# A two-layer transformer with routed experts on one core: second attention in groups of two steps, gates turned, side work in small pieces

## The chip, the core and the metric

The kernel is one program on one core of a Trainium2 chip. The metric is the time of one execution on the device, in microseconds (us). The core has five instruction streams that matter here: TensorE (PE, with its weight loads shown apart as PEld), VectorE (DVE), ScalarE (ACT), GpSimd (POOL) and SyncE (SP, which here issues DMAs only). Each runs its own instructions in order; they meet by semaphores. Results of TensorE go to banks of PSUM, 128 partitions by 512 f32 values each, and a bank can be written again once its reader is through.

## The reference

The input x has 4 batches of 1024 tokens, 256 wide, f32. Two layers follow each other, each `x = x + attention(layernorm(x))` and `x = x + ffn(layernorm(x))`.

The first layer has windowed attention (16 heads of 16, window 64) and a mixture of 8 routed SwiGLU experts, two per token by softmax of `x @ gate_w + gate_b`, beside two shared experts. The second layer is the one that most of the change is about:

```python
def _L1_attn_ref(x, wq, bq, wk, bk, wv, bv, wo, bo, gamma, beta):
    Q = (x @ wq + bq).reshape(B * H, S, D)      # B=4, H=16, S=1024, D=16
    K = (x @ wk + bk).reshape(B * H, S, D)
    V = (x @ wv + bv).reshape(B * H, S, D)
    attn = softmax(einsum('bqd,bkd->bqk', Q, K) / sqrt(D))
    out = einsum('bqk,bkd->bqd', attn, V).reshape(B, S, 256) @ wo + bo + x
    return layernorm(out) * gamma + beta

def _L1_ffn_ref(x, gate_w, experts):
    gates = sinkhorn(einsum('bnd,de->bne', x, gate_w))   # 8 rounds
    vals, idx = top_k(swapaxes(gates, -1, -2), 128)      # 128 tokens per expert and batch
    # x[idx] @ experts[e], times the gate value, put back in the tokens' rows (set), else 0
```

Since the reshape is not followed by a transpose, one "head" of 1024 rows by 16 is 64 token rows in 16 chunks of 16 columns. There are 64 such heads; the kernel takes them in 32 pairs.

## The kernel before

**Stages.** First attention, then the feed-forward part of layer one, then the second attention with the start of the second feed-forward part hidden in it, then a tail: the rest of the routing, the experts and the way back. A tile is 128 tokens (32 tiles, `NT`), a unit four tiles (8 units, `NU`).

**Second attention.** The loop at L2145 runs over steps `s`, eight key tiles (`KT`) for each of 32 pairs of heads (`p`), and one step more. A step does, in this order:

- two halves of `scores` (L1840), one for each 512 query columns. A half takes two banks, one for each of the two heads. It issues two matmuls of `k_st` by `q_st`, with 64 rows each, and two that subtract the row maxima (`minus` by `top_st`). ScalarE then turns each bank into exponentials (L1858), which go into one of six slots of `wide`.
- after each half, one part of `maxima` (L1790) for the step `AHEAD` = 12 later: two matmuls of `q_st` by `k_st`, and their row maxima on VectorE. The first part (`kk` = 0) uses a double bank and one reduction (L1808), the second two single banks and two reductions (L1811). When a pair of heads has all its maxima, `max_rows` (L1816) transposes them, and SyncE stores them to DRAM (`tops_d`) and loads them back as `top_st`.
- the `sums` (L1863) of the step before: 16 matmul instructions with values `v_t` as 32-column weights, all into one accumulator bank (`acc`). These have a tile form of 128 by 32, the scores and maxima 64 by 128.
- `some` (L2008), twice: side work, out of queues of generators. A call advances `between` and `aside` by a piece, then the first of `outs`, `projects`, `gating` that has one, and if it had one (or the flag is set) `sort`.
- at the first key tile, a copy of the accumulator on ScalarE (`oT`, L2175), and a new job in `outs`.

The banks of this stage are `open_banks(one=5, two=1, acc=1)` (L2143): five single ones, one double, one accumulator. Side work takes its banks from the single ones too (`misc_bank`).

**Side work.** `put_out` (L1878) is the output side of one pair: transposes of `oT`, a reciprocal and a product on VectorE that give `ctx`, transposes of that and a copy `cT` on ScalarE, the output projection, and the sum `y` (L1910 on VectorE, L1913 on GpSimd, L1914 on VectorE). A piece ends at each `yield 1`; `yield 0` ends a turn without work. `project` (L1690 and on) computes Q and K of a unit, 512 columns at a time into a pair of banks, stores them to DRAM, from where `load` brings them as `q_st` and `k_st`. `values` does four heads per piece. `finish` is the layernorm after a group of tiles (`TOGETHER`). `gate_steps` computes the gates of the second feed-forward part, `share_steps` the Sinkhorn rounds, `choose_steps` (queue `sort`) the choice of 128 tokens per expert for the first half of the batches: 16 rounds of three VectorE operations. `ranks` then scatters the chosen places into DRAM (`rank_d`), 16 times on GpSimd; `rank` is read back after the loop.

**What sets the order.** In the loop, `on_tensor` (L79) ties each TensorE instruction to the one before, so TensorE runs in the order in which the program is written. `issue_after` puts an instruction behind another in the order of issue and adds no wait. The other engines' order follows from a scheduler that honours these ties.

**Gates.** Both layers' gates are computed with the 128 tokens of a tile as weights and the 8 columns of the gate matrix moving (`gate`, and the end of `gate_steps`):

```python
mm_on(ps[:, j * E : (j + 1) * E], lhsT=xT[:, kc, :], rhs=gw1[:, kc, :], ...)
```

Of the kernel before, what the change touches and what calls it, by code (L numbers as in the profile page):

```python
# [18 lines left out]
P = 128  # L19
# [20 lines left out]
def two_layers(  # L40
# [95 lines left out]
    def one_bank():  # L136

        if "one" in sets:
            return lone_bank("one")
        turns.append(0)  # L140
        return acc_bank() if len(turns) % 2 else misc_bank()
# [41 lines left out]
    first_w.append(first_pool.tile([P, NF, D], F32, name="first2"))  # L183
    gw = first_pool.tile([P, 2, E], F32, name="gw")
    gb = first_pool.tile([P, E], F32, name="gb")
# [33 lines left out]

    def gate(u: int):  # L220
        ps = one_bank()
        for j in range(UT):
            for kc in range(2):
                mm_on(
                    ps[:, j * E : (j + 1) * E],
                    lhsT=wide[:, u, kc, j * P : (j + 1) * P],
                    rhs=gw[:, kc, :],
                    start=(kc == 0),
                    stop=(kc == 1),
                )  # L230
        nc.vector.tensor_tensor(
            logits[:, u * UT : (u + 1) * UT],
            ps[:, : UT * E].rearrange("p (j e) -> p j e", j=UT),
            gb.unsqueeze(1).to_broadcast([P, UT, E]),
            ALU.add,
        )
# [65 lines left out]
    with ExitStack() as lc:  # L302
# [28 lines left out]
        nc.scalar.dma_start(out=wo_t, in_=w_out.rearrange("(k p) e -> p k e", p=P))  # L331
        nc.scalar.dma_start(out=gw, in_=gate0_w.rearrange("(k p) e -> p k e", p=P))
        nc.scalar.dma_start(out=gb, in_=gate0_b.partition_broadcast(P))
# [458 lines left out]

    gw1 = fpool.tile([P, 2, E], F32, name="gw1")
    nc.sync.dma_start(out=gw1, in_=gate1_w.rearrange("(k p) e -> p k e", p=P))

# [447 lines left out]
    def gate_steps(i0: int, i1: int, bank, lag: int):  # L1243

        std = small.tile([P, NT], F32, tag="std", name="std")
        nc.scalar.activation(std[:, i0:i1], mv_all[:, i0:i1, 1], AF.Sqrt, bias=eps_t)
        yield from wait(lag)
        nc.vector.reciprocal(rstd_all[:, i0:i1], std[:, i0:i1])
        yield from wait(lag)
        xns = []  # L1250
        for t in range(i0, i1):
            xn = gpool.tile([P, D], F32, tag="xng", name="xng", bufs=4)
            last_xn[:] = [
                (nc.gpsimd if lag else nc.vector)
                .tensor_scalar(
                    xn, x_t[t], mv_all[:, t, 0:1], rstd_all[:, t : t + 1], ALU.subtract, ALU.mult
                )
                .ins
            ]
            nc.gpsimd.dma_start(out=xn_d[t // TB][(t % TB) * P : (t % TB + 1) * P, :], in_=xn)  # L1260
            xns.append(xn)
            yield 0
        yield from wait(2 * lag)
        xTs = []
        for j in range(0, i1 - i0, 2):
            pair = xns[j : j + 2]
            ps = bank()
            for h, xn in enumerate(pair):
                for kc in range(2):
                    c = (2 * h + kc) * P  # L1270
                    turn_on(ps[:, c : c + P], xn[:, kc * P : (kc + 1) * P], ident)
            xT = gpool.tile([P, 4, P], F32, tag="xTg", name="xTg")
            n = 2 * len(pair)
            nc.scalar.copy(xT[:, :n, :].rearrange("p k t -> p (k t)"), ps[:, : n * P])
            xTs += [xT[:, 2 * h : 2 * h + 2, :] for h in range(len(pair))]
            yield 1
        yield from wait(lag)
        ps = bank()
        for j, xT in enumerate(xTs):
            for kc in range(2):  # L1280
                mm_on(
                    ps[:, j * E : (j + 1) * E],
                    lhsT=xT[:, kc, :],
                    rhs=gw1[:, kc, :],
                    start=(kc == 0),
                    stop=(kc == 1),
                )
        nc.vector.tensor_scalar(
            gates[:, i0:i1, :],
            ps[:, : (i1 - i0) * E].rearrange("p (j e) -> p j e", e=E),  # L1290
            CLIP,
            None,
            ALU.max,
        )
        yield 1

    def share_steps(g: int, bank, lag: int):
# [4 lines left out]
        for _ in range(8):  # L1302
# [15 lines left out]
            nc.vector.tensor_tensor(mine, mine, rsum.to_broadcast([P, GT, E]), ALU.mult)  # L1318
            yield 1

# [299 lines left out]
    with ExitStack() as lc:  # L1620
# [68 lines left out]

        def project(u: int):  # L1690

# [22 lines left out]
            for n, w_t in enumerate(wqk_t):  # L1714
                ps = bank_pair()
                for g in range(2):
                    for kc in range(2):
                        mm_on(
                            ps[g],
                            lhsT=w_t[:, kc, g * P : (g + 1) * P],  # L1720
                            rhs=xnT[:, kc, :],
                            start=(kc == 0),
                            stop=(kc == 1),
                        )
                split = apool.tile([P, 2, 2, UN], F32R, tag="split", name="split")
                for g in range(2):
                    bias = b_col[:, 2 * n + g : 2 * n + g + 1]
                    src = ps[g]
                    nc.scalar.activation(split[:, 0, g, :], src, AF.Identity, bias=bias)
                    nc.vector.scalar_tensor_tensor(  # L1730
                        split[:, 1, g, :], src, bias, split[:, 0, g, :].bitcast(F32),
                        ALU.add, ALU.subtract,
                    )

# [7 lines left out]
                halves[u, n] = d  # L1742
                yield 1

        def values(u: int):
# [4 lines left out]
            nc.gpsimd.memset(v_t.rearrange("p h k c -> p (h k) c")[:, :, DH:], 1.0)  # L1750
            for hq in range(HU // 4):
                ps = misc_bank()
                for hh in range(4):
                    t0 = (4 * hq + hh) * HN

                    for kc in range(2):
# [8 lines left out]
                nc.vector.tensor_tensor(  # L1765
                    v_t[:, 4 * hq : 4 * hq + 4, :, :DH],
                    ps.rearrange("p (h k d) -> p h k d", k=8, d=DH),
                    bv_b.to_broadcast([P, 4, 8, DH]),
                    ALU.add,
                )  # L1770
                yield 1
            vals[u] = v_t
# [17 lines left out]
        def maxima(p: int, j: int, kk: int, tops):  # L1790

            q_st, k_st = q_ring[p % RING], k_ring[p % RING]
            if "one" in sets and kk:
                whole, sc = [], bank_pair()
            else:
                two = two_banks().rearrange("p (h c) -> p h c", h=2)
                whole, sc = [two], [two[:, 0], two[:, 1]]
# [80 lines left out]
        def put_out(i: int, oT):  # L1878
# [16 lines left out]
            )  # L1895
            yield 1
            yield 0
# [4 lines left out]
            nc.scalar.copy(cT.rearrange("p k t -> p (k t)"), ps[:, :D])  # L1902
            yield 1
            yield 0
# [10 lines left out]
            ys.append(y)  # L1915
            yield 1
            if i in TOGETHER:
# [89 lines left out]

        def some(idle: bool):  # L2008

            with ExitStack() as behind:  # L2010
                for ins in newest.values():
                    behind.enter_context(tc.issue_after(ins))
                step(between)
                step(aside)
                if step(outs) or step(projects) or step(gating) or idle:
                    step(sort)

# [68 lines left out]
        def stacks():  # L2086
            roots(0, UT)
            yield
            for did in project(0):
                if did:  # L2090
                    yield
# [50 lines left out]
        before, oT_ps = None, None  # L2142
        open_banks(one=5, two=1, acc=1)  # L2143
        in_turn.append("all")
        for s in range(NP * KT + 1):  # L2145
            p, k = divmod(s, KT)
            if k == 0:
# [7 lines left out]
                if p % UT == 3 and p + 5 < NP:  # L2155
                    all_of(projects)
                    projects.append(project(p // UT + 2))
            if k == 1:
                oT_ps = acc_bank()
            pts = []  # L2160
            due = list(noted)
            noted.clear()
            for half in range(2 if p < NP else 0):
                pts.append(scores(p, k, half))
                maxima_step(s + AHEAD, half)
            for half in range(2 if s else 0):
                sums(*divmod(s - 1, KT), half, before, oT_ps)
            for n in due:
                max_rows(n, top_parts.pop(n))
            for half in range(2):  # L2170
                some(half == 0 and k % 4 == 0)
            before = pts
            if k == 0 and s:
# [4 lines left out]
                )  # L2178
                outs.append(put_out(p - 1, oT))
        in_turn.clear()  # L2180
        open_pairs()
# [172 lines left out]
```

## Time and profile before

| what | value |
|---|---|
| time, three runs | 2254.3, 2247.34, 2251.69 us; median 2251.69 |
| the profiled execution | 2264.11 us; span 2262.3 us |
| mean granted TensorE clock in it | 0.958 |
| first attention | 0 to 336 us, 336 long |
| first layer's feed-forward part | 336 to 1110 us, 774 long |
| second attention, to its last sum | 1110 to 2108 us, 998 long |
| tail | 2108 to 2262 us, 154 long |

All times in the tables of the profile come from one execution, taken by the profiler. Busy time is the union of an engine's instructions; "granted clock" is the TensorE clock that the chip allowed, as a share of full speed. A timeline line gives the start, the length from the first start to the last end, the engine, the source line (L86 and L93 are those of the helper that issues TensorE's instructions, so go by the names of the tiles), the tile written and those read, the shapes and the number of instructions, and in brackets the idle time before and who ended it. In a line of a DMA queue, the first word after the queue is the source line.

### The profile page before, as it was taken

To read this page: it belongs to the slowest core of one execution; us is meant where nothing else is said; L and a number is where in the kernel's file an instruction comes from. 1 tells how busy PE (TensorE), PEld (TensorE's weight loads), DVE (VectorE), ACT (ScalarE), POOL (GpSimd) and SP (SyncE) were. 2 spreads that over 40 slices of the span, in tenths; PEclk is the share of its full clock that TensorE was granted. 3 is DMA by queue.
4 is the path that set the end of the run, shared out by engine and by line. 5 is a ranking of instruction groups with operands and counts; after the bars stand their busy time and mean duration, and the time that the engine had idled before them with its cause. 6 is when DMAs were issued, how large, how long until landed. Compare 5 with 4: busy or idle time off the path is not lost.

```text
span 2262.3 us, 50241 instructions
## 1 busy us (share of the span) xinstructions
PE 2085.9 (92%) x19890; PEld 1378.9 (61%) x19890; DVE 1357.9 (60%) x2702; ACT 997.3 (44%) x1898; POOL 651.8 (29%) x862
## 2 busy tenths in 40 slices
PE   7999999999999999997999999999999999998564
PEld 4777776555788888853555555555555555554341
DVE  6676654522222222245887777777777889994483
ACT  3554542111222222221266666767666656667241
POOL 3656541442000000023421222221131212125555
PEclk9999999999999999998999999999999999999676
DMA  4211106113276677633343113132312122100235
GB/s 146 56 44 45 47 12 199 54 65 128 74 234 223 216 234 227 221 97 84 82 109 69 46 46 70 49 76 49 77 44 63 39 60 47 49 21 12 85 98 163
DMA packets 207015, 212.76 MB, mean 94 GB/s; under 512 B 90024, under 2 KB 166088, under 8 KB 206780
## 3 DMA queue, kind: packets, MB, share of 16 engines
q1 hardware_dynamic: 183996, 169.46, 26.6%
q0 software_dynamic: 11552, 29.72, 4.3%
q10 hardware_dynamic: 11232, 10.37, 1.3%
q8 instruction: 158, 2.59, 0.5%
q14 instruction: 77, 0.63, 0.1%
HBM read 140.70 MB, written 56.96 MB: 87 GB/s over the span
## 4 chain that ended last, share of the span: by engine, by line
PE 72%; DVE 12%; issue 6%; POOL 3%; ACT 3%; DMA 2%; SPq 1%; another core or an unknown queue 0%; ACTq 0%; POOLq 0%; DVEq 0%
PE one L86 32%; PE two L86 12%; PE acc L86 10%; PE two L82 7%; PE misc L86 5%; DVE tops L1811 3%; DVE tops L1808 3%; PE misc L82 2%; PE acc L82 2%; ACT wide L1858 1%; POOL yr L2046 1%; POOL xg L1465 1%; DVE cur L1348 1%; PE two L1531 1%; POOL yr L1584 1%
## 5 line engine op out<-in xcount | busy, mean ns | idle before, releaser
L1858 ACT ACTIVATE wide<-one 128x512 f32<-128x512 f32 x1024 | 529.8, 603 | 233.1 <-PE one L86 225.1
L1808 DVE TENSOR_REDUCE tops<-two 128x2 f32<-128x1024 f32 x268 | 325.4, 1216 | 68.5 <-PE two L86 62.0
L1811 DVE TENSOR_REDUCE tops<-one 128x1 f32<-128x512 f32 x488 | 312.9, 679 | 14.7 <-PE one L86 14.6
L86 PE MATMUL acc<-wide,v_t 128*32 128x256 f32 x4096 | 282.4, 393 | 2.5 <-ACT wide L1858 2.1
L86 PE MATMUL two<-xbT,w_t 128*128 128x256 f32 (+1 forms) x1280 | 253.6, 356 | 1.7 <-ACT xbT L1148 1.4
L86 PE MATMUL one<-q_st,k_st 64*128 64x512 f32 x1024 | 243.9, 451 | 2.8 <-ACT wide L1858 1.7
L86 PEld LDWEIGHTS two<-xbT,w_t 128*128 128x128 f32 x1280 | 221.6, 190 | 29.2 <-ACT xbT L1148 1.8
L1181 DVE SCALAR_TENSOR_TENSOR glu_b<-two,b_blk,act_b 128x256 f32<-128x256 f32 (+1 forms) x160 | 72.7, 454 | 244.0 <-ACT act_b L1174 244.0
L86 PE MATMUL one<-top_st,minus 64*128 64x512 f32 x1024 | 215.0, 399 | 2.6 <-DMA top_st<-tops_d 2.6
L1174 ACT ACTIVATE act_b<-two,b_blk 128x256 f32<-128x256 f32 (+1 forms) x160 | 71.9, 450 | 295.1 <-PE two L86 162.6
L86 PE MATMUL one<-k_st,q_st 64*128 64x512 f32 x488 | 174.2, 457 | 29.9 <-ACT wide L1858 21.8
L86 PEld LDWEIGHTS acc<-wide,v_t 128*32 128x32 f32 x4096 | 108.4, 110 | 116.2 <-issue 63.9
L86 PEld LDWEIGHTS one<-q_st,k_st 64*128 64x128 f32 x1024 | 104.7, 186 | 97.2 <-ACT wide L1858 41.7
L271 ACT ACTIVATE act<-two,bT 128x512 f32<-128x512 f32 x60 | 41.2, 687 | 263.9 <-PE two L82 258.4
L86 PEld LDWEIGHTS one<-k_st,q_st 64*128 64x128 f32 x488 | 86.2, 186 | 111.4 <-ACT wide L1858 77.8
L2046 POOL DMA_INDIRECT yr<-ys_d,slot x64 | 61.9, 968 | 222.1 <-DMA ys_d<-yb 80.5
L86 PE MATMUL misc<-w_t,glu_b 128*128 128x256 f32 x552 | 125.6, 379 | 0.0
L82 PE MATMUL two<-wide,w_t 128*128 128x512 f32 x256 | 118.0, 616 | 4.1 <-DVE tops L1808 3.1
L1231 POOL TENSOR_TENSOR x<-x,sb_b 128x256 f32<-128x256 f32 x32 | 23.2, 725 | 336.0 <-DVE glu_b L1181 336.0
L601 POOL TENSOR_SCALAR_AFFINE_SELECT pT<-pT 64x512 f32<-64x512 f32 x128 | 84.0, 656 | 111.9 <-ACT pT L591 109.8
L1913 POOL TENSOR_TENSOR y<-y,wide 128x256 f32<-128x256 f32 x32 | 23.3, 729 | 303.1 <-DVE y L1910 270.6
L86 PEld LDWEIGHTS one<-top_st,minus 64*128 64x128 f32 x1024 | 102.3, 188 | 12.5 <-DMA top_st<-tops_d 2.9
(411 smaller groups left out, 3429.0 us busy)
## 6 DMA issues: line engine op xcount, KB each, us to landing
w_t<-in_L_ffn_rw_dram SPq DMA_DIRECT2D x120, 512.0 KB
halves<-split SPq DMA_DIRECT2D x64, 256.0 KB
q_st<-halves SPq DMA_DIRECT2D x128, 128.0 KB
k_st<-halves SPq DMA_DIRECT2D x256, 64.0 KB
xb<-xs_d SPq DMA_DIRECT2D x31, 256.0 KB
ys_d<-yb ACTq DMA_DIRECT2D x31, 256.0 KB
xs_d<-zeros SPq DMA_DIRECT2D x5, 1536.0 KB
b_t<-in_L_ffn_rb_dram SPq DMA_DIRECT2D x40, 128.0 KB
```

Source lines behind the costliest of these rows:

```text
L82: return do(*args, **kw)
L86: done = do(*args, **kw)
L271: nc.scalar.activation(act, ps[0], AF.Silu, bias=bT[0][:, f, e : e + 1])
L601: nc.gpsimd.affine_select(out=part, in_=part, compare_op=ALU.is_ge, fill=0.0, base=0, pattern=[[0, 8], [1, WIN]], channel_multiplier=-1,)
L1174: nc.scalar.activation(act[:, :cols], ps[:, ff * cols : (ff + 1) * cols], AF.Silu, bias=b_blk[0][:, f, n : n + 1],)
L1181: nc.vector.scalar_tensor_tensor(glu[:, f, :cols], ps[:, 512 + ff * cols : 512 + (ff + 1) * cols], b_blk[1][:, f, n : n + 1], act[:, :cols ...
L1231: nc.gpsimd.tensor_tensor(x_t[m], x_t[m], sb3_b, ALU.add).ins, newest_glu[0]
L1808: last = nc.vector.tensor_reduce(tops[:, :, j, kk], whole[0], AX.X, ALU.max)
L1811: last = nc.vector.tensor_reduce(tops[:, hh, j, kk : kk + 1], sc[hh], AX.X, ALU.max)
L1858: newest["scalar"] = nc.scalar.activation(pt[:, hh * 512 : (hh + 1) * 512], sc[hh], AF.Exp).ins
L1913: nc.gpsimd.tensor_tensor(y, y, bo_b, ALU.add)
L2046: ga = nc.gpsimd.indirect_dma_start(out=yr[:, :], out_offset=None, in_=ys_d[:, :], in_offset=bass.IndirectOffsetOnAxis(ap=slots[k][:, i : ...
```

## The change

- **Gates turned.** The gate matrices `gw` and `gw1` are widened to 32 columns with zeros and become the weights; the tokens move. Four tiles take the four 32-column strips of TensorE, each writing 32 partitions of one bank (`gates_across`). ScalarE copies the result to SBUF, and one TensorE transpose turns it back (`gates_down`).
- **All banks single.** The stage opens `one=7, acc=1`; both parts of `maxima` take two single banks, with two reductions.
- **Groups of two steps.** The loop advances two steps at a time: first half of step one, maxima, `max_rows` if due, `some` once, second half of step one, two parts of maxima, the sums of the two steps before in one run (32 instructions), the copy `oT` where due, first half of step two, maxima, second half of step two.
- **Small pieces.** Each `yield` gives a size instead of 1. `project` works in pieces of 256 columns with one bank each, `values` in pieces of two heads. `some` takes up to four pieces, and no more once their sizes reach 1.2; `sort` moves at the first of its four turns, and at the third if more than 0.8 is spent. In the preparation before the loop `project(0, 1)` keeps the former size.

```diff
-    gw1 = fpool.tile([P, 2, E], F32, name="gw1")
-    nc.sync.dma_start(out=gw1, in_=gate1_w.rearrange("(k p) e -> p k e", p=P))
+    gw1 = fpool.tile([P, 2, 32], F32, name="gw1")
+    nc.vector.memset(gw1, 0.0)
+    nc.sync.dma_start(out=gw1[:, :, :E], in_=gate1_w.rearrange("(k p) e -> p k e", p=P))
...
+    def gates_across(ps, w, tokens):
+        for kc in range(2):
+            for j, of in enumerate(tokens):
+                mm_on(ps[32 * j : 32 * j + 32, :P], lhsT=w[:, kc, :], rhs=of(kc),
+                    start=(kc == 0), stop=(kc == 1), skip_group_check=True)
+        across = small.tile([P, P], F32, tag="across", name="across")
+        rows = slice(0, 32 * len(tokens))
+        nc.scalar.copy(across[rows], ps[rows, :P])
+        return across
+
+    def gates_down(ps, across, n: int):
+        rows = slice(0, 32 * n)
+        turn_on(ps[:, rows], across[rows], ident[rows, rows])
+        return ps[:, rows].rearrange("p (j c) -> p j c", c=32)[:, :, :E]
...
-        def project(u: int):
+        def project(u: int, parts: int = 2):
...
-                ps = bank_pair()
-                for g in range(2):
-                    for kc in range(2):
-                        mm_on(ps[g], ..., rhs=xnT[:, kc, :], ...)
+                pair = bank_pair() if parts == 1 else None
...
+                    for part in range(parts):
+                        cols = slice(part * UN // parts, (part + 1) * UN // parts)
+                        src = pair[g] if pair else misc_bank()[:, cols]
+                        for kc in range(2):
+                            mm_on(src, ..., rhs=xnT[:, kc, cols], ...)
...
+                        if parts > 1:
+                            yield 0.85
...
-            for hq in range(HU // 4):
+            for hp in range(HU // 2):
                 ps = misc_bank()
-                for hh in range(4):
+                for hh in range(2):
...
-                yield 1
+                yield 0.85
...
         def maxima(p: int, j: int, kk: int, tops):
-            if "one" in sets and kk:
+            if "two" not in sets:
                 whole, sc = [], bank_pair()
...
         def put_out(i: int, oT):   # after ctx, after cT, after y
-            yield 1
+            yield 0.45
...
-            yield 1
+            yield 0.25
...
-            yield 1
+            yield 0.85
...
-        def some(idle: bool):
-            with ExitStack() as behind:
-                for ins in newest.values():
-                    behind.enter_context(tc.issue_after(ins))
-                step(between)
-                step(aside)
-                if step(outs) or step(projects) or step(gating) or idle:
-                    step(sort)
+        def some():
+            spent = 0
+            for turn in range(4):
+                with ExitStack() as behind:
+                    for ins in newest.values():
+                        behind.enter_context(tc.issue_after(ins))
+                    step(between)
+                    step(aside)
+                    if spent < 1.2:
+                        spent += step(outs) or step(projects) or step(gating)
+                    if turn == 0 or (turn == 2 and spent > 0.8):
+                        step(sort)
...
-        open_banks(one=5, two=1, acc=1)
+        open_banks(one=7, acc=1)
         in_turn.append("all")
-        for s in range(NP * KT + 1):
+        for s in range(0, NP * KT + 1, 2):
...
-            for half in range(2 if p < NP else 0):
-                pts.append(scores(p, k, half))
-                maxima_step(s + AHEAD, half)
-            for half in range(2 if s else 0):
-                sums(*divmod(s - 1, KT), half, before, oT_ps)
+            half_step(0, 0)
+            maxima_step(s + AHEAD, 0)
             for n in due:
                 max_rows(n, top_parts.pop(n))
-            for half in range(2):
-                some(half == 0 and k % 4 == 0)
+            some()
+            half_step(0, 1)
+            maxima_step(s + AHEAD, 1)
+            maxima_step(s + 1 + AHEAD, 0)
+            if s:
+                for j in range(2):
+                    pb, kb = divmod(s - 2 + j, KT)
+                    if kb == 0:
+                        oT_ps = acc_bank()
+                    for half in range(2):
+                        sums(pb, kb, half, before[j], oT_ps)
             before = pts
             if k == 0 and s:
                 oT = work.tile([P, 4, 2, HN], F32, tag="oT", name="oT1", bufs=2)
...
                 outs.append(put_out(p - 1, oT))
+            half_step(1, 0)
+            maxima_step(s + 1 + AHEAD, 1)
+            half_step(1, 1)
```

`half_step(j, half)` appends `scores(p, k + j, half)` to the results of step `j` as long as `p < NP`.

## The prediction

> **What bounds the kernel now.** I read the page first, then the busy time by stage, then the timeline of single steps in the stage that the change rewrites, engine by engine, and last the waits of the SyncE queue near the end.
>
> ```profile
> span 2262.3 us, 50241 instructions
> ...
> PE 2085.9 (92%) x19890; PEld 1378.9 (61%) x19890; DVE 1357.9 (60%) x2702; ACT 997.3 (44%) x1898; POOL 651.8 (29%) x862
> ```
>
> The averages hide four stages. The third row below is the second attention, the fourth what follows its last sum (columns: length, then busy time and instructions of PE, PEld, DVE, ACT, POOL, then granted clock, DMA share, GB/s).
>
> ```profile
> 1110.00:2108.00 998.00, 951.97 (x8315) 548.16 (x8311) 784.92 (x1305) 652.65 (x1226) 249.15 (x283) 0.97 0.24 56
> 2108.00:2262.00 154.00, 73.95 (x398) 46.51 (x394) 91.66 (x191) 36.35 (x72) 85.44 (x98) 0.68 0.42 126
> ```
>
> 998 us for 256 steps. One step with no side work, on PE (start, length, and at the end of the line the count):
>
> ```profile
> 1502.78 1.07 PE L86 MATMUL acc<-wide,v_t 128*32 128x256 f32 x16
> 1503.78 0.50 PE L86 MATMUL one<-q_st,k_st 64*128 64x512 f32 x2
> 1504.12 0.40 PE L86 MATMUL one<-top_st,minus 64*128 64x512 f32 x2
> 1504.35 0.39 PE L86 MATMUL two<-k_st,q_st 64*128 64x512 f32 x2
> 1504.58 0.40 PE L86 MATMUL one<-q_st,k_st 64*128 64x512 f32 x2
> 1504.81 0.40 PE L86 MATMUL one<-top_st,minus 64*128 64x512 f32 x2
> 1505.04 0.72 PE L86 MATMUL one<-k_st,q_st 64*128 64x512 f32 x2
> 1505.69 1.07 PE L86 MATMUL acc<-wide,v_t 128*32 128x256 f32 x16
> ```
>
> Sums to sums 2.91 us; 102 of 254 steps have no side work, and 2.91 is their median. A pair of 64-row matmuls costs 0.23 in a row, the sums 4 rounds of 0.216 (starts 1502.78, 1503.02, 1503.23, 1503.45). That is 6 x 0.23 + 4 x 0.216 = 2.26. The rest: about 0.2 into the sums, 0.11 + 0.10 out of them (the changes of tile form), and 0.22 because the last pair's second head starts at 1505.26, not 1505.04. What it waits for is ScalarE (its timeline):
>
> ```profile
> 1504.61 2.06 ACT L1858 ACTIVATE wide<-one 128x512 f32<-128x512 f32 x4 [0.84 <-PE one L86]
> 1512.50 2.06 ACT L1858 ACTIVATE wide<-one 128x512 f32<-128x512 f32 x4
> ```
>
> and on PE, a step later:
>
> ```profile
> 1513.15 0.50 PE L86 MATMUL one<-k_st,q_st 64*128 64x512 f32 x1 [1.90 <-ACT wide L1858]
> ```
>
> An exp begins 0.50 after its minus matmuls start (1504.12 to 1504.61), exps follow each other every 0.515 (2.06 / 4), and a bank is free 0.65 after its exp starts (1512.50 to 1513.15). Added up: first exp 0.34 + 0.50 = 0.83 after the sums' end, bank free at 1.48, 0.43 to the sums, 1.00 of sums: 2.91. So the step is a chain through PE and one exp, not PE alone. VectorE:
>
> ```profile
> 1506.55 1.28 DVE L1811 TENSOR_REDUCE tops<-one 128x1 f32<-128x512 f32 x2
> 1507.74 1.22 DVE L1808 TENSOR_REDUCE tops<-two 128x2 f32<-128x1024 f32 x1
> ```
>
> A single-bank maximum goes every 0.595 ((1507.74 - 1506.55) / 2), a double one 1.13.
>
> **The change, part by part. A pair of steps without side work.** One entry and exit of the sums goes: 0.41 per pair; a run of two steps lasts 1.00 + 4 x 0.216 = 1.86. PE alone would need 4 score half-steps (1.86), 4 pairs of maxima (0.93), 0.31 around the sums and 8 rounds (1.73), 0.1 of form: 4.97 against 5.82 for two steps now. But all scores and maxima now draw on one ring of seven banks, so a bank waits for the reader of the seventh allocation back, and I walk that. T = 0 is the first q matmul after the sums. Exps of step two's halves start at 0.83, 1.35, 1.86, 2.38; those of the next pair's first half-step, with ScalarE never idle, at 2.89 and 3.41. The last frees its bank at 4.06, and by the ring that is the bank of the third pair of maxima before the next sums. They start 0.43 later, at 4.49, and end at 6.35. So an empty pair takes 6.35, not 4.97: +0.53 on 5.82. ScalarE works 4.12 of that; it starves while two steps' sums run. VectorE needs 8 x 0.595 = 4.76 (now 4.6) and isn't the chain.
>
> **Pairs with side work.** All side matmuls of a pair now stand in one place, after the first half-step's maxima (PE there at 2.23; its bank is free at 2.39). About 1 us of them fits into the wait for the exps. The order of PE's instructions in the changed kernel gives the counts for some 122 pairs; costs of pieces now are step lengths less 2.91 (medians: oT 3.50, ctx 3.28, output projection 3.97, maxima's transposes 3.11, sixteen q/k matmuls 10.13, all values 8.17).
> - 14 empty pairs: 14 x 0.53 = +7.4.
> - 17 light ones (the turn-back of the gates, one group of xn transposes, a column sum): one extra bank shifts the ring, 6.59 against about 6.14: +7.7.
> - 17 with oT and ctx in the same run. PE is in order, and the ctx transposes need the reciprocal and product on VectorE, which stand behind two maxima (free at 3.69): 3.69 + 0.29 + 0.42 + 0.05 = 4.45; 0.37 of transposes; then 3.0 to the end: 7.85. Now these lie in different steps: 5.82 + 0.59 + 0.37 = 6.78. 17 x 1.07 = +18.2. Ends: 0 if VectorE runs them ahead of the maxima; 2.3 where a sort operation (1.2 us) is queued between the two, as in five of them.
> - 65 heavy pairs (projections, values, outputs): PE-bound, 5.2 plus pieces against 5.82 plus pieces, less about 0.35 for entering and leaving the side work twice: 52 x -0.3, and 13 x -0.1 where the output projection waits for the copy of cT in its own run (ScalarE reaches it at 4.17): -17.
> - 13 of these or light pairs hold the addition on VectorE that waits for GpSimd's 0.73 (y at L1914; 17 such waits now, 12.3 us): it is now ahead of four maxima, not three spread out. Between 0 and 1.4 each; I take 0.7: +9.
> - Gate matmuls of the second layer: now 16 instructions with 128-column weight loads, (xn and gates 5.18, less 2.91 and 0.43) 1.84. Then four concurrent 32-column tiles, 4 rounds of about 0.11, and two changes of form. 6 x -1.0 = -6. In layer one the same, but the turn-back follows at once and PE waits for the ScalarE copy: 1.8 now, 1.6 to 2.1 then; 8 x 0 (0.3 either way).
>
> Sum of the stage: +19. The eight table-load stalls of each kind stay: a 2.9 us detour of ScalarE (1.28 + 0.30 + 1.28) delays either chain by about 1.5.
>
> **The clock.** In the trace the clock halves only after a stretch of 3.4 us with long PE gaps: after the 1.90 us above, granted 0.94 over 1512 to 1568, and 1.00 where gaps stay under about a microsecond. My walk leaves three gaps of 0.1, so I price no halving; oT and ctx pairs have 1.3 in one piece, the upper end below. The Trainium skill ("TensorE: Matmul & The Clock Gate", A second HAM failure mode) says that PE cycling through PSUM banks with short idles makes the clock swing between full and half, which speaks against a ring that is waited on in every pair. By that rule one half-speed window per pair would add 122 x 1.7 = 207 us, to some 2480; no row here shows it for gaps this short.
>
> **The end.** The sort of the first half of the gates gets one or two turns per pair, not up to two per step: by the instruction order some ten of sixteen rounds (30 x 1.25 = 37 us) stand after the last maximum, and are over about when the sums are (about 40 us then). The 16 scatters of ranks (1.25 apart) move behind the last sum, VectorE's read of them stands inside the eight share rounds of the second half: 3 to 5 late, 1.5 of its own work, 1.5 for the gates' extra copy and transpose: +8. Against it, this wait goes, since the load of ranks no longer stands on SP ahead of the last top_st load (PE without scores, 2071 to 2078.5):
>
> ```profile
> SPq L1603 <- DMA rank_d<-place,at_i: 28.7, 2, 21.0
> ```
>
> -6.5. Net +1.5.
>
> Total +19 + 1.5 = +21. The profiled execution took 2264.11 (span 2262.3 and 1.8 around it), 12.4 above the median of 2251.69; the differences are put on the median: 2272.
>
> **Rivals.** (A) Faster: VectorE and GpSimd keep ahead of PE, so that in-run waits vanish (+18.2 becomes -5, +9 becomes 0), and table loads hide under the double sums (16 x -0.6): 21 - 23 - 9 - 10 = -21, 2231; if light pairs gain too (6.1, not 6.59), -15 more. For it: PE has 95% of the stage, and 0.41 of form changes per pair surely goes. Against: the 1.48 us chain above. (B) Slower still: the clock halves after each 1.3 us gap: 17 x 1.7 = +29, 2301. It decides once gaps near 1.3 suffice. (C) What is saved in heavy pairs equals what is lost in light ones: within 0.3%, 2245 to 2258.5, which is about what a measurement of this kernel can tell from no change.
>
> **How the numbers follow.** My sum, 2259 to 2290: 0.41. A and below: 0.33. B: 0.18. C: 0.08. So faster 0.33, same 0.08, slower 0.59. For 8 in 10 the range goes down to A with 10 more (2220) and up to B with 10 more (2312). My sum's own range is 2259 to 2290.
>
> **What would show it.** Empty pairs 6.35 apart (4.97 to 5.8: my ring walk is wrong and A holds); ScalarE idle 2.1 in one piece at the sums; PE waiting for VectorE at ctx in 17 pairs; the sums as 32 matmuls in 1.86; sorting after the last maximum; granted clock of the stage at 0.97 or above (below 0.94: B). If the stage is under 980 us I am wrong in sign.

## The result and the profile after

The changed kernel took 2266.92 us (median of 4 runs, 2263.62 to 2269.04) against 2251.39 for the kernel before: ratio 1.0069, 95% interval 1.0048 to 1.009. Measured once more beside the experiments it took 2281.58 against 2268.91: 1.0054, interval 1.0034 to 1.0073. So it is slower by 12.7 to 15.5 us, under 1%; the forecast was +20.3 on the median. The kernel before itself took 2251.4 in the first measurement and 2266.7 to 2268.9 in the later ones, so only ratios are compared from one measurement to the other.

The page of the changed kernel:

```profile
span 2261.9 us, 50831 instructions
...
PE 2054.6 (91%) x20020; PEld 1373.5 (61%) x20020; DVE 1385.1 (61%) x2992; ACT 995.3 (44%) x1944; POOL 653.6 (29%) x862
```

The spans of the two profiled executions are equal, although the medians are not: the one of before was 12.4 above its median, this one 3.3 below. The stages are therefore read against a second profile as well, that of an experiment whose work ahead of and behind the loop is that of before (before_single). From the trace of each kernel, in us: start is the time of the first matmul of scores, loop the length from there to the end of the last sum, tail what follows:

| kernel | start | loop | tail |
|---|---|---|---|
| before | 1110.5 | 998.0 | 153.8 |
| after, first profile | 1098.6 | 1009.5 | 153.9 |
| after, second profile | 1097.2 | 1012.7 | 167.8 |
| before_single | 1110.8 | 964.9 | 158.9 |

So the loop lost 11.5 to 14.7, and the start came 12 to 14 earlier. The tail lost 9 in the later series of runs (167.8 against 158.9) and nothing in the first pair of profiles (153.9 against 153.8).

Below, a group is two steps of the loop, measured from one run of sums to the next; an empty group, or empty pair, has no side work. The side work of a unit repeats every 16 groups, some 122 us, which is called a cycle. An empty pair in the changed kernel, on PE and on ScalarE (timeline):

```profile
1285.31 1.93 PE L86 MATMUL acc<-wide,v_t 128*32 128x256 f32 x32
1287.17 0.50 PE L86 MATMUL one<-q_st,k_st 64*128 64x512 f32 x2
1287.50 0.40 PE L86 MATMUL one<-top_st,minus 64*128 64x512 f32 x2
1287.73 0.40 PE L86 MATMUL one<-k_st,q_st 64*128 64x512 f32 x2
1287.96 0.40 PE L86 MATMUL one<-q_st,k_st 64*128 64x512 f32 x2
...
1290.11 1.48 PE L86 MATMUL one<-k_st,q_st 64*128 64x512 f32 x4
1291.52 1.29 PE L86 MATMUL acc<-wide,v_t 128*32 128x256 f32 x20
```

```profile
1287.99 4.03 ACT L1875 ACTIVATE wide<-one 128x512 f32<-128x512 f32 x8 [2.25 <-PE one L86]
```

6.21 from sums to sums, the run of 32 matmuls 1.86, ScalarE idle 2.25 in one piece; the last four maxima take 1.48 where two pairs of 0.23 would do, because they wait for banks. The waits that changed most, in a list of TensorE's waits over 1110 to 2110, before and after:

```profile
PE one L86 <- ACT wide L1858: 23.5, 16, 1.9
PE one L86 <- DVE y L1914: 3.8, 5, 2.3
PE one L86 <- DVE ctx L1890: 1.1, 3, 0.5
```

```profile
PE one L86 <- DVE ctx L1907: 38.0, 17, 7.3
PE one L86 <- DVE y L1931: 19.2, 8, 3.0
PE one L86 <- DVE tops L1828: 3.1, 9, 1.0
PE one L86 <- ACT wide L1875: 2.5, 3, 2.0
```

(Columns: us in all, times, longest.) Two waits for VectorE have grown, and most of the waits for ScalarE's exps have gone. The second of the grown ones is no matter of VectorE itself, which waits for GpSimd there (VectorE's list over the same time, before and after):

```profile
DVE y L1914 <- POOL y L1913: 12.3, 17, 0.8
```

```profile
DVE y L1931 <- POOL y L1930: 49.6, 20, 5.9
```

At a group that follows a layernorm (timeline of GpSimd, VectorE, TensorE):

```profile
1398.48 1.41 POOL L1964 TENSOR_TENSOR y<-y,wide 128x256 f32<-128x256 f32 x2
1399.85 1.40 POOL L1965 TENSOR_TENSOR x<-x,y 128x256 f32<-128x256 f32 x2
1401.21 0.72 POOL L1930 TENSOR_TENSOR y<-y,wide 128x256 f32<-128x256 f32 x1
```

```profile
1401.96 0.42 DVE L1931 TENSOR_TENSOR y<-y,one 128x256 f32<-128x256 f32 x1 [5.93 <-POOL y L1930]
1402.30 1.28 DVE L1828 TENSOR_REDUCE tops<-one 128x1 f32<-128x512 f32 x2
```

```profile
1402.44 0.50 PE L86 MATMUL one<-q_st,k_st 64*128 64x512 f32 x2 [3.04 <-DVE y L1931]
```

The bias of y (L1930) stands on GpSimd behind the layernorm chain of two tiles; VectorE waits 5.93 for it, with all maxima behind; TensorE runs out of banks and waits 3.04. That group, with the gates' matmuls, takes 11.3; six groups of the loop have this wait.

### The profile page after: what moved, and what is told of

Same layout as the page of the kernel before. It is cut to its first block, busy times and chain, and to the rows that moved or that the text cites. A ratio compares the mean times of both kernels' runs of the same rounds, so it can differ in the third digit from the quotient of the medians.

```text
span 2261.9 us, 50831 instructions
## 1 busy us (share of the span) xinstructions
PE 2054.6 (91%) x20020; PEld 1373.5 (61%) x20020; DVE 1385.1 (61%) x2992; ACT 995.3 (44%) x1944; POOL 653.6 (29%) x862
## 4 chain that ended last, share of the span: by engine, by line
PE 66%; DVE 11%; issue 10%; POOL 7%; DMA 3%; ACT 3%; SPq 0%; POOLq 0%; ACTq 0%; DVEq 0%
PE one L86 29%; PE acc L86 13%; PE two L86 11%; PE two L82 6%; DVE tops L1828 4%; PE misc L82 2%; PE acc L82 2%; POOL y L1960 1%; ACT wide L1875 1%; POOL yr L2067 1%; DMA yr<-ys_d,slot 1%; DVE top_v L1420 1%; DVE cur L1420 1%; PE misc L86 1%; POOL y L1964 1%
## 5 line engine op out<-in xcount | busy, mean ns | idle before, releaser
L1828 DVE TENSOR_REDUCE tops<-one 128x1 f32<-128x512 f32 x976 | 614.7, 681 | 116.7 <-PE one L86 116.2
L86 PE MATMUL one<-q_st,k_st 64*128 64x512 f32 x1024 | 286.1, 475 | 24.6 <-DVE y L1931 19.0
L86 PE MATMUL acc<-wide,v_t 128*32 128x256 f32 x4096 | 261.1, 396 | 1.6 <-ACT wide L1875 1.6
L86 PE MATMUL one<-top_st,minus 64*128 64x512 f32 x1024 | 252.3, 415 | 0.0
L86 PE MATMUL one<-k_st,q_st 64*128 64x512 f32 x976 | 221.8, 433 | 3.3 <-DVE tops L1828 1.7
L86 PEld LDWEIGHTS one<-q_st,k_st 64*128 64x128 f32 x1024 | 123.4, 189 | 163.8 <-DVE tops L1828 51.7
L86 PEld LDWEIGHTS acc<-wide,v_t 128*32 128x32 f32 x4096 | 123.3, 113 | 121.0 <-issue 56.0
L86 PEld LDWEIGHTS one<-k_st,q_st 64*128 64x128 f32 x976 | 115.2, 193 | 62.2 <-ACT wide L1875 34.4
L1930 POOL TENSOR_TENSOR y<-y,wide 128x256 f32<-128x256 f32 x32 | 23.2, 727 | 365.7 <-DVE y L1927 310.6
L86 PE MATMUL acc<-w_t,glu_b 128*128 128x256 f32 x552 | 125.6, 379 | 0.0
L86 PEld LDWEIGHTS acc<-w_t,glu_b 128*128 128x128 f32 x552 | 101.9, 190 | 12.3
```

The source lines that it names most:

```text
L86: done = do(*args, **kw)
L1828: last = nc.vector.tensor_reduce(tops[:, hh, j, kk : kk + 1], sc[hh], AX.X, ALU.max)
L1930: nc.gpsimd.tensor_tensor(y, y, bo_b, ALU.add)
```

## The experiments

Five rounds each. The ratios are to the kernel before, run in the same series. Where a ratio to the changed kernel is named, it is that ratio divided by 1.0054, which was measured in the series of after_again, before_single, gates_back and spread; for the others it is carried over from there.

**after_again**: the changed kernel, unedited.

> The changed kernel itself, unedited, beside the kernel before on the chip of these runs, on which the kernel before took 2267.1 and not 2251.4. Theory 1 (the extra 15 us lie in the tail, which is 168 to 172 long in the four runs before and 154 in the two first profiles, and the cost of the change lies in the loop): ratio 1.005 to 1.009, some 2278 to 2287 us, loop 1008 to 1011, tail 168 to 172. Theory 2 (the cost of the change depends on the chip): ratio 0.998 to 1.003.

Ratio 1.0054 (1.0034 to 1.0073); loop 1012.7, tail 167.8. Theory 1, with the loop 1.7 beyond its range.

**ctx_later**

```diff
-            yield 0.45
-            yield 0
+            yield 0.45
+            yield from next_round()   # yields 0 until some() is called again
```

> The changed kernel with one edit: after the transposes of oT, the output job waits for the next group of two steps before it transposes ctx, so that VectorE has a whole pair for the reciprocal and the product. Theory 1 (TensorE, in order, stands still at the ctx transposes because VectorE is behind two to four maxima or sort operations: 38.0 us in 17 waits in the trace after): the 17 waits go; a pair with oT alone takes about 6.9 instead of 8.46, the next one about 7.1 instead of 6.63, so -1.1 x 17 = -18, and the late ones with sort operations (10.0 to 16.1 long) give up to 15 more: 2232 to 2250 us against 2266.9. Theory 2 (TensorE would wait for a bank or for ScalarE at that point anyway, the ctx wait only covers it): 2260 to 2268, and the pairs stay near 8.

Ratio to before 0.9989 (0.9976 to 1.0001), 0.9935 to the changed kernel, or -15. The loop fell by 23 to 26, to 986.6, and of the 17 waits for ctx one is left (38.0 us before, 2.3 now). The groups with oT alone took 6.45 (forecast 6.9), those after them 8.3, where 7.1 was expected: they now hold the ctx transposes, the copy cT and the projection, and TensorE's waits for cT rose from 2.3 us to 12.1 in 25 times. Theory 1, with a gain just short of its range (2232 against 2266.9 is 0.985, 2250 is 0.9925).

**y_early**

```diff
         def put_out(i: int, oT):
+            y = pool.tile([P, D], F32, tag="y", name="y", bufs=5)
+            nc.vector.tensor_scalar(y, x_t[i], ..., ALU.subtract, ALU.mult)
+            nc.gpsimd.tensor_tensor(y, y, bo_b, ALU.add)
             ps = misc_bank()
...
-            y = pool.tile(...)        # the same three, after the output projection
```

> The changed kernel with one edit: the first two operations of y (normalization on VectorE, bias on GpSimd) are issued with the transposes of oT, not after the output projection. Theory 1 (the 11.3 to 11.8 us pairs at the gates are long because the bias addition stands on GpSimd behind two tiles' layernorm chain, VectorE waits 5.9 us for it with the maxima behind, and TensorE 3.0 us): five of these pairs fall to about 7, -4.5 x 5 = -22, and the 24 waits of 0.4 to 0.85 give 0 to 5 more: 2240 to 2247 us against 2266.9. Theory 2 (those pairs are long because of the turned gates and their ScalarE copy): they stay at 11 and the time at 2264 to 2268.

Ratio 0.9969 (0.9957 to 0.998), 0.9915 to the changed kernel, or -19; loop 986.1. The gate groups fell from 11.3 to 6.45 with the gates still turned. Theory 1, at the edge of its range; theory 2 is out. Something was lost elsewhere: one group of the cycle rose from 7.6 to 9.0, and TensorE's waits for the layernorm statistics (mv_all) from 1.9 us once to 11.7 in 5 times.

**ctx_y**: both edits.

> The changed kernel with the edits of ctx_later and y_early together. Theory 1 (the loop costs 45 us more than with single banks alone because of two queues that the bunched side work makes: VectorE behind maxima at ctx, GpSimd behind the layernorm chain at y; they are separate, each was worth 23 us of loop): loop about 964 to 970, as long as that of before_single (964.9), so that the grouping of the sums itself costs or gains nothing that shows; with the start at 1098 and the tail at 168 to 172 the ratio to before is 0.987 to 0.993. Theory 2 (both edits only move one and the same wait): loop 980 to 987, ratio 0.996 to 0.999.

2228.37 us, ratio 0.983 (0.9814 to 0.9846). The loop is 951.4, shorter than either theory said and 58 to 61 below the changed kernel's, 9 to 12 more than the two gains added. That surplus is about what the clock can give: the stretches at half speed inside the loop add up to 85.3 and 92.2 us in the two profiles after, 64.9 in each of ctx_later and y_early, 23.9 here (58.0 before). So the two edits together took away 14 to 21 us more of them than each alone, added up; at half speed that is up to 7 to 10 us of TensorE time. Over 1100 to 2060 the granted clock was 0.96 after (first line) and 0.99 here (second; last columns: clock, DMA share, GB/s):

```profile
1100.00:2060.00 960.00, 893.85 (x8088) 537.82 (x8083) 768.03 (x1506) 613.15 (x1199) 215.64 (x244) 0.96 0.23 57
```

```profile
1100.00:2060.00 960.00, 921.13 (x8467) 549.52 (x8465) 807.03 (x1586) 642.54 (x1262) 239.05 (x272) 0.99 0.24 60
```

**before_single**: the kernel before with single banks alone.

```diff
-            if "one" in sets and kk:
+            if "two" not in sets:
...
-        open_banks(one=5, two=1, acc=1)
+        open_banks(one=7, acc=1)
```

> The kernel before with one part of the change alone: seven single banks and two single reductions per part of the maxima; steps, sums and side work as before. Theory 1 (the ring of seven is no cost by itself; what costs is where the maxima stand ahead of the sums, which stays as before here): steps without side work 2.9, time within 0.3% of before. Theory 2 (a shared ring with scores and maxima is the cost): empty steps 3.1 to 3.2, that is +0.25 x 102 = +25 at least, ratio 1.01 or more. It also shows a second profile of the first two stages as they were before: the loop starting at about 1099 means that the 1110.5 of the first profile was that run's own.

Neither theory: 2236.25 us, ratio 0.9852 (0.9836 to 0.9867), -33 us, all of it in the loop (964.9). Empty steps stayed at 2.91. What went are the stalls at ScalarE's table loads. TensorE's waits for exps, 23.5 us before, are now:

```profile
PE one L86 <- ACT wide L1858: 1.1, 2, 0.6
```

That is 22 of the 33. With these stalls the half-speed stretches in the loop fell from 58.0 to 21.0 us, up to 18 us of TensorE time. One such place (timeline, ScalarE and TensorE):

```profile
1498.53 1.28 ACT L1934 ACT_TABLE_LOAD   x1
1499.83 0.30 ACT L1934 ACTIVATE std<-mv,eps_t 128x4 f32<-128x4 f32 x1
1500.14 1.28 ACT L1858 ACT_TABLE_LOAD   x1
1501.44 1.09 ACT L1858 ACTIVATE wide<-one 128x512 f32<-128x512 f32 x2
```

```profile
1499.56 0.39 PE L86 MATMUL one<-top_st,minus 64*128 64x512 f32 x2
1499.79 0.98 PE L86 MATMUL one<-k_st,q_st 64*128 64x512 f32 x2
1500.70 1.07 PE L86 MATMUL acc<-wide,v_t 128*32 128x256 f32 x16
```

Before, the last maxima of such a step waited 1.90 for an exp, the line at 1513.15 in the prediction. Here the second of the two starts at 1500.27, ahead of any exp after the load and just after a reduction has ended: it has a bank that a reduction freed. With five banks for scores and one part of the maxima none such was to be had there. The largest gap on TensorE within 6 us of a table load is 1.4 to 1.9 at most of the loads before, 0.1 at most of them here and after.

**before_single_gates**: before_single with the gates of both layers turned, as in the change.

> The kernel before with single banks (before_single) and the gates of both layers turned; steps, sums and side work as before. Theory 1 (the forecast: -1.0 at each of six gate pieces, nothing in the first layer): -3 to -8 on before_single, ratio to before 0.9815 to 0.984. Theory 2 (gates_back, +20 on the changed kernel, shows their worth everywhere): -20, ratio 0.976. Theory 3 (the separate piece for the turn-back costs as much as is saved): 0 to +4.

2223.09 us, ratio 0.9802 (0.9786 to 0.9819), 0.9949 to before_single, or -11: between theories 1 and 2, and the fastest of all. In the loop the gate step fell from 5.18 to 4.07 and the turn-back's step is 3.15 against 2.91, as forecast; the loop as a whole stayed (964.7), while half-speed stretches in it rose from 21.0 to 36.4, up to 8 us. The profile shows the gain at the start (1105.6 for 1110.8) and in the tail (155.0 for 158.9).

Beside ctx_y, from the same series, its loop is 13 longer (964.7 against 951.4) and its tail 18 shorter (155.0 against 173.3). So with the two waits gone, the regrouping does gain in the loop; what it loses is in the tail.

**gates_back**: the changed kernel with the gates as before.

> The changed kernel with the gates of both layers as before (tokens as weights, no copy, no transpose back). Theory 1 (the forecast: turned gates save 1.0 each in the second layer, nothing in the first): +6, ratio to the changed kernel 1.001 to 1.004. Theory 2 (the turn-back costs what the fewer rounds save, since its pair is a pair of its own and 6.45 long): -6 to 0, since six pairs have one piece less. Theory 3 (the gate pairs are 11.3 to 11.8 long because of it): -25, which y_early speaks against (the pairs fell to 6.45 with the gates still turned).

Ratio 1.0141 (1.0123 to 1.0159), 1.0087 to the changed kernel, +20: more than theory 1. By the profile +11 of it is in the loop, +5 at the start, +2 in the tail. Inside the loop the main place is the group with the gates and the wait for y: 14.4 to 14.7 against 10.7 to 11.9, and 7.7 against 6.45 for the one behind it. Why the other form of the matmuls costs some 3 there, and not the 1.0 of the forecast, was not followed further.

**two_runs**

```diff
             if s:
-                for j in range(2):           # sums of both steps
+                ...                          # sums of the first step only
+            half_step(1, 0)
+            maxima_step(s + 1 + AHEAD, 1)
+            if s:
+                ...                          # sums of the second step
```

> The changed kernel with the grouping of the sums alone undone: the sums of the first step of the pair before stand where they are now, those of the second after the first half of step two and its maxima, so two runs of 16 matmuls instead of one of 32. Theory 1 (the long run starves ScalarE, which costs more in empty and light pairs than the saved 0.41 of form changes): empty pairs 5.8 to 6.0 instead of 6.62, light ones and those with oT and ctx 0.5 less each, pairs with much side work 0.3 more each; 48 x -0.6 + 65 x 0.3 = -9: 2250 to 2264 us against 2266.9. Theory 2 (the saved form changes are what the change gains, and the bank order costs nothing): 0.41 x 122 = +50: about 2310.

Ratio 1.0107 (1.009 to 1.0124), 1.0053 to the changed kernel, +12, of which the profile has 5 to 8 in the loop (1017.3). Both theories fall: the saved form changes are worth at most a quarter of 50, and empty pairs did not get shorter (6.26 against 6.21 to 6.25). What makes an empty pair long is not the run of 32 matmuls.

**one_maximum_first**

```diff
+            maxima_step(s + AHEAD, 0)
             half_step(0, 0)
-            maxima_step(s + AHEAD, 0)
+            maxima_step(s + AHEAD, 1)
...
             half_step(0, 1)
-            maxima_step(s + AHEAD, 1)
             maxima_step(s + 1 + AHEAD, 0)
```

> The changed kernel with one edit in the order of TensorE: one of the two parts of maxima that stand right ahead of the sums moves to the front of the group (maxima, half, maxima, side work, half, maxima, sums, half, maxima, half). Theory 1 (an empty pair is 6.62 and not the 5.0 of TensorE alone because the last maxima before the sums need the bank of the last exp, seven allocations back): the walk with the same steps gives 0.56 less per pair, so 6.0 to 6.1 for empty pairs, -0.5 for some 50 empty and light pairs, nothing for the 65 with much side work: 2240 to 2252 us against 2266.9. Theory 2 (VectorE's eight reductions or ScalarE's idle time at the sums set the 6.62): empty pairs stay at 6.5 to 6.7, time within 4 us.

Ratio 1.0206 (1.0189 to 1.0222), +34 on the changed kernel: the forecast of the whole was wrong, that of the empty pair right (5.82 for 6.21). So the order of the banks in front of the sums is the cause there. But the side work now stood behind two parts of maxima on VectorE, and a new wait came in 30 groups:

```profile
PE one L86 <- DVE ctx L1907: 36.3, 17, 3.1
PE one L86 <- DVE top L1836: 22.9, 30, 0.8
PE one L86 <- DVE y L1931: 13.0, 7, 2.2
```

**spread**: maxima, half, side work, maxima, half, maxima, sums, half, maxima, half.

> The changed kernel with another order of TensorE: maxima, first half of step one, side work, maxima, second half, maxima, sums, first half of step two, maxima, second half. As in one_maximum_first no two parts of maxima stand next to each other ahead of the sums, but only one part, not two, stands between the sums and the side work. Theory 1 (two parts of maxima right before the sums wait for the bank of the last exp; the side work suffers only when two parts of maxima stand ahead of it): empty pairs 5.8 to 5.9 as in one_maximum_first, pairs with side work as in the changed kernel or up to 0.3 less: some 45 x -0.4 = -18, ratio to the changed kernel 0.988 to 0.995. Theory 2 (the first half of step one must come first to feed ScalarE, whatever the order of the rest): ratio 1.005 or more.

Ratio 1.0028 (1.0017 to 1.004), 0.9974 to the changed kernel, -6: between the theories. Empty pairs 5.82 as expected, but the groups with q/k matmuls took 0.2 to 0.45 more each (7.54 for 7.30, 8.78 for 8.32).

**ctx_y_spread**

> ctx_y with the order of maxima of spread. Theory 1 (empty and light pairs are bound by the bank ring, which spread cuts from 6.27 to 5.90, and the gain was partly lost there in the waits that ctx_y takes away): -8 to -20 on ctx_y, ratio to before 0.979 to 0.988, which would be the fastest of all. Theory 2 (spread moves a wait for a bank to one for VectorE in pairs with side work, 7.54 for 7.31 in the pairs of q and k): within 5 us of ctx_y.

This is ctx_y with the order of spread. Ratio 0.9899 (0.9879 to 0.992), 13 slower than ctx_y: against theory 1, and by more than the 5 of theory 2, in theory 2's direction. A cycle of 16 groups took 120.5 against 117.0; the empty pairs were 0.4 shorter, the groups with ctx, cT and the output projection up to 2.7 longer.

**ctx_y_sort2**

```diff
-                        spent += step(outs) or step(projects) or step(gating)
-                    if turn == 0 or (turn == 2 and spent > 0.8):
+                        spent += step(outs) or step(gating) or step(projects)
+                    if turn in (0, 2):
```

> ctx_y with two edits to the side work's queues: gating goes ahead of projects, and sort moves at the first and third turn of every group whatever was spent. All 48 operations of the sort then stand ahead of the last maximum, as in the kernel before, and the scatters of ranks can go while the loop runs. Theory 1 (the changed kernel's tail of 168 to 173 against 155 to 159 comes from the late sort: scatters 13 to 33 us after the last sum instead of before it, share rounds 26 long instead of 20): tail 154 to 160, that is -14 on ctx_y, against +5 to +15 in the loop (951.4) for some 30 sort operations of 1.25 that now stand in busy groups: loop 956 to 967, ratio 0.977 to 0.984. Theory 2 (the tail is long for another reason, the turned gates of the last tiles or the chip): tail 168 or more, ratio 0.985 or more.

2244.03 us, ratio 0.9907 (0.9891 to 0.9923). The tail is as theory 1 said: 159.0 against 173.3, with the scatters 84 to 26 us ahead of the last sum instead of 17 to 37 behind it. A late sort does not always cost that much: in the first profile of the changed kernel the scatters lie 13 to 34 us behind the last sum and the tail is 153.9, and why is open. The loop rose by 31.5, to 982.9, not by 5 to 15: by these two edits together more is lost between the maxima than is won at the end. Half-speed stretches in the loop rose with it, from 23.9 to 51.2 us. How much of the 31.5 belongs to the sort and how much to the other order of gating was not tried.

## Why the prediction was right, and where its steps were not

The total was right, in good part by luck: terms that were not in the sum cancel. The loop lost 11.5 to 14.7 where +19 was forecast, and the start came 12 earlier where nothing was. Inside the loop, the -33 of the single banks was not forecast; it offset two waits that cost more than their terms.

- **Empty and light pairs.** Forecast 6.35 and 6.59; measured 6.21 to 6.25 with no table load near, 6.62 with one, and 6.45 to 6.70. The starving of ScalarE, forecast 2.1, was 2.25. The bank that the last maxima wait for is confirmed by two orders (5.82 each). The expectation of two_runs drew a link from there to the length of the sums' run; that was wrong: two_runs leaves 6.26. (The prediction's terms for TensorE alone add up to 4.93, not 4.97, on which nothing rests, and the kinds of pairs it lists make 113 of its 122.)
- **oT and ctx in one run.** The mechanism was right; +18.2 was too small. Forecast 7.85 a pair, 7.9 measured where nothing else is queued, but 8.46 in the median, and 10 to 16 where sort operations or a wait for GpSimd stand ahead on VectorE. Undone, it gives 23 to 26 of loop. The longest wait is near the end (VectorE and TensorE):

```profile
2085.16 1.19 DVE L1360 MATCH_REPLACE8 cur<-top_v,cur 16x1024 f32<-16x1024 f32 x1
2086.28 0.40 DVE L1907 TENSOR_TENSOR ctx<-one,rec 128x256 f32<-128x256 f32 x1
```

```profile
2086.83 0.66 PE L86 MATMUL one<-ident,ctx 128*128 128x128 f32 x2 [7.30 <-DVE ctx L1907]
```

- **The addition that waits for GpSimd.** The mis-sized term: "Between 0 and 1.4 each; I take 0.7: +9". Six of these waits were 5.9 long, and moving the addition gave 23 to 27 of loop. The step that failed looked at the 0.73 of the operation and not at what is ahead of it in GpSimd's queue once four turns of side work are issued in one place.
- **Heavy pairs.** -17 forecast. In a cycle the eight groups with q/k and values took 60.2 after, the 16 steps in the same place 64.35 in before_single; less the 1.84 of gate matmuls that stand elsewhere after, that is -2.3 a cycle, some -16 over seven cycles. Right.
- **Table loads.** "The eight table-load stalls of each kind stay" is the step that failed on the other side: they went with the double bank, -33 in before_single, about 22 of it waits and the rest no more than the clock can give. The Trainium skill ("ScalarE: Activation LUTs", What ACT_TABLE_LOAD costs) puts a switch at 2.66 us with a drain of 1.38, so some 5.3 for there and back. The trace has 2.9 (1.28 + 0.30 + 1.28, and the next exp 0.02 later), and the measurement decides.
- **Gates.** -1.0 each in the second layer: 1.11, less 0.24 for the turn-back. In the first layer 0 was forecast; both profiles with the gates turned alone or put back alone show 4 to 5 us at the start.
- **The start.** Not forecast: 12 us earlier. 4 to 5 of it go with the gates; in the rest VectorE's order differs. Before, four reductions of maxima stand behind an addition that waits 3.07 for a gathered row, and TensorE waits for them (first two lines); after, they stand ahead of it (third line). That the scheduler's order is all of the rest was not tried.

```profile
1046.41 0.48 DVE L2060 SCALAR_TENSOR_TENSOR x<-yr,weight,x 128x256 f32<-128x256 f32 x1 [3.07 <-DMA yr<-ys_d,slot]
1048.06 4.61 DVE L1808 TENSOR_REDUCE tops<-two 128x2 f32<-128x1024 f32 x4
```

```profile
1042.75 4.61 DVE L1825 TENSOR_REDUCE tops<-two 128x2 f32<-128x1024 f32 x4
```

- **The clock.** No halving was priced. Half-speed stretches in the loop rose from 58.0 to 85.3 us, some 14 us at most, so part of rival B came about, and the granted clock of the stage was 0.96, not the 0.97 or above of the forecast. The long gaps went ahead of it: after the wait of 3.04 above, half clock over 1404.4 to 1407.8. Waits for banks in every round alone did not do it: ctx_y has them too (empty pairs 6.22) and no half-speed stretch from the start of its loop to 1769. The rule on bank cycling that the prediction weighed, with its +207, is not borne out for such short waits.
- **The end.** Tail +8 forecast, +9 measured in the later series, by the mechanism named, and nothing in the first pair of profiles. The -6.5 for the load of ranks was given back: the 7.30 above stands where TensorE stood still before.

Rival A's condition (VectorE and GpSimd ahead of TensorE) is what ctx_y comes near to, and the result is beyond the 2231 given to it, relative to before: 0.983 of 2251.69 would be 2213.

## What to carry to other kernels

When side work is gathered in one place per round, look at every in-order queue that it is issued to, not only at the matrix engine's: an operation of 0.73 behind another job's chain of 6 us stops the engine that waits for it, and then the one that waits for that. Give a result that crosses two engines a whole round before its next step, and issue what depends on nothing new early. Measure the parts of a bundled change alone: here single banks (-33 us) and turned gates (-11) were gains, and the regrouping took both back. The groups of two steps and the small pieces of side work in it were not measured apart.

## What was not expected of the hardware

- Waits cost twice: the longer gaps on TensorE are mostly followed by 3.4 to 10.2 us at half clock. In the two loops of before and after, such a stretch began within 4 us after none of 21 gaps of 0.3 to 1.2 us, 7 of 18 of 1.2 to 1.8, and 25 of 27 longer ones. Taking away two waits worth 23 to 27 us each gave 58 to 61 together.
- A bank layout with the same number of banks decides whether a 2.9 us detour of ScalarE reaches TensorE: a gap of 1.4 to 1.9 with five single banks and a double one, 0.1 with seven single ones, at most of the loads.
- The tail of the same kernel took 153.9 in one profile and 167.8 in another. Up to the last Sinkhorn round, 45 us after the last sum, the two run alike; the last gather of tokens for the experts is issued 117 us after the last sum in one, 131 in the other. What makes the difference was not found.
